# A graph layer's output product with the operands exchanged: rank sums stationary, W2 moving

## The chip, the cores and the metric

The kernel runs on one core of a Trainium2 chip. The metric is the device time of one execution in microseconds (us). A measurement of this kernel repeats within a fraction of a percent: the three runs of the kernel before lie between 972.28 and 972.99 us, with a median of 972.44 us.

Five engines work side by side, each on its own queue of instructions: TensorE (PE, with its weight loads listed apart as PEld), VectorE (DVE), ScalarE (ACT), GpSimd (POOL) and SyncE (SP, which here issues the DMAs). They wait for one another through semaphores.

## The reference

There are 128 graphs of 128 nodes with 64 features. The first layer is an edge network, the second a weighted sum over neighbours.

```python
# layer 0
h = relu(layernorm(x))                         # no scale, no shift
mask = (adj > 0)
t[b,j,k,:] = relu(h[b,j] @ W1a + (h[b,j] - h[b,k]) @ W1b + b1)   # 192 hidden channels
hm[b,j,:] = sum over k of t[b,j,k,:] * mask[b,j,k]
x1 = x + hm @ W2 + deg[b,j] * b2               # W2 is 192 x 64
# layer 1
h2 = relu(layernorm(x1))
out = x1 + (adj @ h2) @ W.T
```

The change touches `hm @ W2` and the addition that makes `x1` from it.

## The kernel before

**Groups and jobs.** The graphs are worked on in 32 groups of G = 4. In a group, each node's neighbours are ranked within each quarter of the 128 nodes, and the first D = 6 of a quarter get a slot. A *job* builds pre-activations for one half of the nodes (64) and two of the four quarters. `Job.fill` (L852) multiplies stacked projections `k3` by one-hot slots `S3` and adds the node's own part, into a PSUM tile `g`. `Job.drain` (L873) empties it. For the first 128 hidden channels (kind 0, one graph) DVE reduces the absolute values into `hm0` (L880). For the last 64 channels (kind 1, two graphs beside each other on the partitions) ACT writes the rectified values into `T` (L890), and POOL adds them up into `hm1`. A group has 24 jobs, numbered t = 0 to 23: 16 of kind 0 and 8 of kind 1; t = 4, 5, 10, 11, 16, 17, 22 and 23 are of kind 1. Edges that found no slot go another way (`pre_edge_*`, `edge_x`, `edge_sum`), through `et`, `R`, `RT` and `X`.

**What runs between the jobs.** While group g's jobs run, pieces for group g+1 (table `AHEAD`, L909) and for group g-1 (table `BEHIND`, L927) are put between them, at the job number that is their key. Those that matter here:

- `pre_proj(g+1, 0)` after t = 7 and `pre_proj(g+1, 1)` after t = 12 (L552): PE writes projections into a PSUM tile `pp`, which comes from the same three buffers as the jobs' `g`. ACT copies a first bfloat16 part (`ca<-pp`), makes `z` (four) and `e` (two); DVE forms `rest` from `pp` and that part; ACT makes the second part (`ca<-rest`); POOL the third (two `ca<-rest,ca`).
- `pre_edge_a` after t = 9: `pv` on PE, `ovf` and `mid` on DVE, four `et<-iov,mid` on ACT. `pre_edge_b` after t = 19: four `et<-et,half` and one `R<-et` on ACT.
- `edge_sum` after t = 1 and `edge_sum1` after t = 4: they end with `u0` (128 hidden channels x 4 graphs x 128 nodes) and `u1` (64 channels of two graphs on 128 partitions x 2 x 128 nodes), the sums over neighbours with hidden channels on the partitions.
- `post0` after t = 8 and `post1` after t = 10: described below. `post2` (L804, after t = 15): `sdb` on ACT, `rsb` and `mrb` on DVE, four `h<-x,mrb,rsb` on ACT. `post3` after t = 16: `pga` on PE and `agg` on ACT. `post4` after t = 19: `po` on PE, `ot` on DVE, the store.

**The product before.** `post0` (L769) holds `w2h` (half of W2's first 128 rows, 128 x 64) and `w2bd` (the last 64 rows twice on a block diagonal, 128 x 128) stationary and lets `u0` and `u1` move, 256 columns at a time. The product `py` then has output features on the partitions; ACT copies it to `ys` in SBUF. `post1` (L790) transposes `ys` twice on PE into `pty`, so that nodes are on the partitions, DVE adds `e` (which holds x and the parts that are linear in h) to give `x1`, and the sums of the layer norm follow (`stb`, `mvb`).

**Buffers.** `gtile` (L237) has 3 buffers of two PSUM banks each, shared by the jobs' `g` and by `pp`: a job can be filled only when a buffer has been drained. `mtile` (L240) has 2 buffers of one bank, for all the small products (`py`, `pty`, `pga`, `po`, `px` and others).

**What sets the order.** PE's instructions stand as they are written. After the first group's preparation `Engine.held` is set to False (L1016), and from there on a scheduler in the framework puts the instructions of DVE, ACT, POOL and SP in order when the program is built; each engine then works its list strictly from the front. The first group and the last have job orders of their own (L963 to L972); the 30 groups between them have the same one, and the built program has the same order of ACT's instructions in all 30.

The helpers `mm`, `tp` and `Engine.call` record every instruction, so that the profile gives nearly all of them the lines 181, 184 and 198; the tile names tell them apart.

Of the kernel before, what the change touches and what calls it, by code (L numbers as in the profile page):

```python
# [8 lines left out]
F32 = mybir.dt.float32  # L9
BF16 = mybir.dt.bfloat16  # L10
I32 = mybir.dt.int32
AF = mybir.ActivationFunctionType
ALU = mybir.AluOpType
# [137 lines left out]
def kernel(  # L151
# [28 lines left out]
    def mm(*args, **kw):  # L180
        return tc.keep_in_program_order(nc.tensor.matmul(*args, **kw))  # L181

    def tp(*args, **kw):
        return tc.keep_in_program_order(nc.tensor.transpose(*args, **kw))  # L184

    class Engine:
# [4 lines left out]
        def __init__(self, engine):  # L191
            self.engine = engine
# [10 lines left out]
    vec, act, pool, sp = (Engine(e) for e in (nc.vector, nc.scalar, nc.gpsimd, nc.sync))  # L203

    B, N, F = x.shape
    H = W1.shape[1]
    O = W2.shape[1]
    P = 128
    G = 4
# [18 lines left out]
    with ExitStack() as main:  # L228
# [4 lines left out]
        tmp = main.enter_context(tc.tile_pool(name="tmp", bufs=2))  # L233
# [3 lines left out]
        def gtile(name):  # L237
            return ps_g.tile([P, 2, 512], F32, tag="g", name=name)

        def mtile(name):  # L240
            return ps_m.tile([P, 512], F32, tag="m", name=name)
# [7 lines left out]
        w2bd = const.tile([P, 2, O], F32, tag="w2bd", name="w2bd")  # L249
        wl1 = const.tile([P, P], F32, tag="wl1", name="wl1")  # L250
        ident = const.tile([P, P], F32, tag="ident", name="ident")
# [20 lines left out]
        for q in range(Q):  # L272
            s = slice(q * QN, (q + 1) * QN)
# [35 lines left out]
        w2h = const.tile([C0, O], F32, tag="w2h", name="w2h")  # L309
# [69 lines left out]
        def bc(t, n, axis):  # L379
            shape = list(t.shape)  # L380
            shape.insert(axis, n)
            return t.unsqueeze(axis).to_broadcast(shape)


        def norm_a(src, u):
            st = tmp.tile([P, G, 6], F32, tag="st", name=f"st{u}")
            mv = tmp.tile([P, G, 2], F32, tag="mv", name=f"mv{u}")
            for b in range(G):
                vec.bn_stats(st[:, b, :], src[:, b, :])
            for b in range(G):  # L390
                vec.bn_aggr(mv[:, b, :], st[:, b, :])
            return mv
# [27 lines left out]
        def keep_busy(tile, n):  # L420
            for _ in range(n):
                mm(tile, oneb, bc(oneb, 4, 1), start=True, stop=True, skip_group_check=True)

        def pre_adj(g, busy=0):
            d = groups[g]
            pt = mtile(f"pt{g}")
            keep_busy(pt, busy)
            for b in range(G):
                tp(pt[:, b * N : (b + 1) * N], d["adj"][:, b, :], ident)
            d["adjT"] = grp.tile([P, G, N], F32, tag="adjT", name=f"adjT{g}", bufs=3)  # L430
            if g == 0:
                pre_norm(0)
            act.activation(
                d["adjT"].rearrange("k b j -> k (b j)"), pt, AF.Copy
            )
            if g < 2:
                return
            pre_mask(g)

        def pre_mask(g):  # L440
            d = groups[g]
            d["maskT"] = grp.tile([P, G, N], BF16, tag="maskT", name=f"maskT{g}", bufs=3)
            vec.tensor_scalar(d["maskT"], d["adjT"], 0.0, -1.0, ALU.is_gt, ALU.mult)
            if "mv" not in d:
                d["mv"] = norm_a(d["x"], f"a{g}")

        def pre_norm(g):
            d = groups[g]

            d["h"] = tmp.tile([P, 2, 2, F], F32, tag="h", name=f"h{g}", bufs=1)  # L450
            norm_b(d["x"], d["mv"], lambda b: d["h"][:, b % 2, b // 2, :], f"a{g}", d.get("scales"))

        def pre_rank(g, busy=0):
            d = groups[g]
            pq = mtile(f"pq{g}")
            keep_busy(pq, busy)
            mm(
                pq, triq, d["maskT"].rearrange("k b j -> k (b j)"), start=True, stop=True
            )
            d["qs"] = grp.tile([P, G, N], BF16, tag="qs", name=f"qs{g}")  # L460
            qf = d["qs"].rearrange("k b j -> k (b j)")
            act.activation(qf, pq, AF.Copy)

            d["ov"] = grp.tile([P, G, N], BF16, tag="ov", name=f"ov{g}")
            vec.tensor_scalar(d["ov"], d["qs"], float(D) + BIG, None, ALU.is_ge)
# [56 lines left out]
                d["hT"].rearrange("p r n -> p (r n)"), ph[:, 0 : 2 * N], AF.Copy  # L522
            )

        def pre_count(g, busy=0):
            d = groups[g]

            pd = mtile(f"pd{g}")
            keep_busy(pd, busy)
            for b in range(G):  # L530
                mm(
                    pd[:, b : b + 1], d["maskT"][:, b, :], negb, start=True, stop=True
                )
                mm(
                    pd[:, G + b : G + b + 1], d["ov"][:, b, :], oneb[:, 0:1], start=True, stop=True
                )
            d["dn"] = grp.tile([P, 2, G], F32, tag="dn", name=f"dn{g}")
            vec.tensor_copy(d["dn"].rearrange("j t b -> j (t b)"), pd[:, 0 : 2 * G])

            d["ns"] = grp.tile([P, G], F32, tag="ns", name=f"ns{g}")  # L540
            vec.scalar_tensor_tensor(
                d["ns"], pd[:, G : 2 * G], float(Q * D), d["dn"][:, 0], ALU.add, ALU.subtract
            )

            d["half"] = tmp.tile([P, G], F32, tag="half", name=f"half{g}")
            vec.tensor_scalar(
                d["half"], pd[:, G : 2 * G], -0.5, 0.5, ALU.mult, ALU.add
            )
            d["nb"] = tmp.tile([P, G], BF16, tag="nb", name=f"nb{g}")
            vec.tensor_copy(d["nb"], pd[:, G : 2 * G])  # L550
# [217 lines left out]

        def post0(g):  # L769
            d = groups[g]  # L770
            py = mtile(f"py{g}")
            d["py"] = py
            for p in range(2):
                s = slice(p * O, (p + 1) * O)
                mm(
                    py[s, 0 : 2 * N], w2h,
                    d["u0"][:, 2 * p : 2 * p + 2].rearrange("h r j -> h (r j)"),
                    start=True, stop=False, skip_group_check=True,
                )
            w = w2bd.rearrange("h p o -> h (p o)")  # L780
            mm(
                py[:, 0 : 2 * N], w, d["u1"].rearrange("h r j -> h (r j)"),
                start=False, stop=True, skip_group_check=True,
            )
            d["ys"] = tmp.tile([P, 2, N], F32, tag="ys", name=f"ys{g}", bufs=1)
            act.activation(
                d["ys"].rearrange("p r j -> p (r j)"), py[:, 0 : 2 * N], AF.Copy
            )

        def post1(g):  # L790
            d = groups[g]
            pt = mtile(f"pty{g}")
            for r in range(2):
                tp(pt[:, r * N : (r + 1) * N], d["ys"][:, r], ident)
            d["x1"] = grp.tile([P, G, F], F32, tag="x1", name=f"x1{g}")
            vec.tensor_tensor(
                d["x1"].rearrange("j (p r) o -> j r p o", p=2),
                pt[:, 0 : 2 * N].rearrange("j (r p o) -> j r p o", r=2, p=2),
                d["e"].rearrange("j (p r) o -> j r p o", p=2),
                ALU.add,  # L800
            )
            d["mv"] = norm_a(d["x1"], f"b{g}")

# [30 lines left out]


        class Job:
            def __init__(self, g, kind, b, jh, qp, busy):
                self.g, self.kind, self.b, self.jh, self.qp = g, kind, b, jh, qp
                self.gt = gtile(f"g{g}_{kind}_{b}_{jh}_{qp}")
                keep_busy(self.gt[:, 0], busy)  # L840

                if kind == 0:
                    self.parts = [(b, slice(0, C0), slice(0, P))]
                else:
                    self.parts = [
                        (2 * p + b, slice(C0, H), slice(p * C1, (p + 1) * C1)) for p in range(2)
                    ]
# [80 lines left out]
            0: (slot_sum,),  # L928
            1: (edge_sum,),
            4: (edge_sum1,),  # L930
            8: (post0,),
            10: (post1,),
            15: (post2,),
            16: (post3,),
            19: (post4,),
# [85 lines left out]
        for g in range(NG):  # L1021
            if 0 < g < NG - 1:
                load(g + 1)
            order = ORDER0 if g == 0 else ORDERL if g == NG - 1 else ORDER
            for t, args in enumerate(order):
                job = Job(g, *args, busy=0)
                job.fill()
                job.drain()
                if g == 0 and t in FIRST:
                    FIRST[t](0)  # L1030
                pieces(OWN, t, g)
                pieces(BEHIND, t, g - 1)
                pieces(AHEAD if g else AHEAD0, t, g + 1)
# [37 lines left out]
```

## Time and profile before

| | |
|---|---|
| median of three runs | 972.44 us |
| the profiled execution | 972.88 us |
| span of its instructions | 971.2 us, mean granted PE clock 0.994 |
| DVE busy | 796.4 us (82% of the span) |
| ACT busy | 698.9 us (72%) |
| POOL busy | 743.1 us (77%) |
| ACT `ys<-py` | 32 times, 0.427 us each at the median |
| one group, from one group's first `py` to the next one's | 474.88 to 504.01 us: 29.1 us |

How to read it. The span counts from the first instruction to the last; the time of the execution is a little longer. A row of the timeline has the start in us, the time from the first start to the last end of the merged instructions, the engine, the operation, the tiles written and read, the number merged, and in brackets the idle time before and what ended it. A matmul is listed with the time from its start until its result stands in PSUM; several overlap. So four `g<-id,k` matmuls are listed with 0.49 us together, while the next instruction begins 0.33 us after the first of them. A short wait of PE is covered by such an overlap and does not show as idle time; the starts have to be compared. For DVE and ACT, too, an instruction can begin about 0.1 us before the listed end of the one ahead of it.

### The profile page before, as it was taken

To read this page: it belongs to the slowest core of one execution; us is meant where nothing else is said; L and a number is where in the kernel's file an instruction comes from. 1 tells how busy PE (TensorE), PEld (TensorE's weight loads), DVE (VectorE), ACT (ScalarE), POOL (GpSimd) and SP (SyncE) were. 2 spreads that over 40 slices of the span, in tenths; PEclk is the share of its full clock that TensorE was granted. 3 is DMA by queue.
4 is the path that set the end of the run, shared out by engine and by line. 5 is a ranking of instruction groups with operands and counts; after the bars stand their busy time and mean duration, and the time that the engine had idled before them with its cause. 6 is when DMAs were issued, how large, how long until landed. Compare 5 with 4: busy or idle time off the path is not lost. (4 is left out here: it accounts for less than half of the span.)

```text
span 971.2 us, 26764 instructions
## 1 busy us (share of the span) xinstructions
PE 945.9 (97%) x10007; PEld 692.5 (71%) x10008; DVE 796.4 (82%) x1880; ACT 698.9 (72%) x1732; POOL 743.1 (77%) x1130
## 2 busy tenths in 40 slices
PE   6899999999999999999999999999999999999995
PEld 2667777777777767777777777777777777777774
DVE  6788888888888888888888888888888888888863
ACT  4867787767787767787767787767787767787752
POOL 1388787778787778787778787778787778787793
PEclk9999999999999999999999999999999999999998
DMA  3655676655676655676655676655676655666510
GB/s 99 132 128 126 150 166 137 148 128 124 145 165 144 138 127 128 147 163 144 138 128 128 146 163 137 145 129 127 146 164 144 140 126 126 147 154 138 123 46 14
DMA packets 88294, 129.91 MB, mean 134 GB/s; under 512 B 47200, under 2 KB 63968, under 8 KB 88160
## 3 DMA queue, kind: packets, MB, share of 16 engines
q1 hardware_dynamic: 87584, 127.98, 57.8%
q8 instruction: 81, 1.33, 0.6%
q14 instruction: 53, 0.43, 0.1%
q10 hardware_dynamic: 576, 0.16, 0.1%
HBM read 13.01 MB, written 4.19 MB: 18 GB/s over the span
## 5 line engine op out<-in xcount | busy, mean ns | idle before, releaser
L198 POOL TENSOR_TENSOR T<-T 128x192 f32<-128x192 f32 (+2 forms) x768 | 526.3, 692 | 97.2 <-ACT T L198 57.2
L198 DVE TENSOR_REDUCE hm<-g 128x64 f32<-128x768 f32 x512 | 476.8, 947 | 81.2 <-PE g L181 79.5
L181 PEld LDWEIGHTS <-k 96*128 96x128 bf16 (+1 forms) x6144 | 411.0, 103 | 177.1 <-issue 51.3
L181 PE MATMUL g<-S,k 96*128 96x384 bf16 (+1 forms) x2048 | 381.9, 330 | 4.7 <-DVE hm L198 3.5
L181 PE MATMUL g<-id,k 96*128 96x192 bf16 (+1 forms) x4096 | 379.8, 246 | 0.0
L198 ACT ACTIVATE T<-g 128x768 f32<-128x768 f32 x256 | 209.5, 820 | 74.5 <-PE g L181 70.2
L198 POOL TENSOR_TENSOR ca<-rest,ca 128x384 bf16<-128x384 f32 x126 | 112.5, 913 | 103.7 <-ACT ca L198 101.2
L198 ACT ACTIVATE ca<-pp 128x768 bf16<-128x768 f32 x64 | 51.4, 803 | 56.0 <-PE pp L181 56.0
L198 DVE TENSOR_TENSOR rest<-pp,ca 128x768 f32<-128x768 f32 x64 | 60.8, 949 | 14.6 <-ACT e L198 14.0
L198 ACT ACTIVATE ca<-rest 128x768 bf16<-128x768 f32 x64 | 55.2, 862 | 22.2 <-DVE rest L198 22.2
L198 DVE TENSOR_SCALAR S<-qs 128x512 bf16<-128x512 bf16 x186 | 71.0, 434 | 0.0
L181 PE MATMUL pe<-RT,X 128*64 128x128 f32 (+1 forms) x512 | 70.5, 280 | 0.0
L181 PE MATMUL pp<-wp,hT 64*128 64x448 f32 x256 | 67.0, 600 | 0.4 <-DVE bias L198 0.4
L198 ACT ACTIVATE z<-pp,ns 128x128 f32<-128x128 f32 (+1 forms) x256 | 65.9, 348 | 0.0
L198 ACT ACTIVATE et<-et,half 128x128 f32<-128x128 f32 x128 | 57.0, 449 | 0.0
L198 ACT ACTIVATE qs<-pq 128x512 bf16<-128x512 f32 x32 | 19.1, 597 | 52.2 <-PE pq L181 50.4
L181 PEld LDWEIGHTS pe<-RT,X 128*64 128x64 f32 (+1 forms) x512 | 52.7, 165 | 5.4 <-issue 5.4
L181 PE MATMUL px<-ca,S 128*128 128x192 bf16 x384 | 52.7, 246 | 0.0
L181 PE MATMUL px<-ca,R 128*128 128x192 bf16 x384 | 52.6, 246 | 0.0
L198 ACT ACTIVATE h<-x,mrb,rsb 128x64 f32<-128x64 f32 x128 | 51.6, 478 | 1.0 <-DVE mrb L198 1.0
L198 ACT ACTIVATE h<-x,mra,rsa 128x64 f32<-128x64 f32 x128 | 48.6, 432 | 1.8 <-issue 1.3
L181 PE MATMUL pe<-ident,z 128*128 128x128 f32 x192 | 49.6, 286 | 0.0
(128 smaller groups left out, 1208.3 us busy)
## 6 DMA issues: line engine op xcount, KB each, us to landing
S<-S SPq DMA_DIRECT2D x372, 192.0 KB, 4.1
k<-ca SPq DMA_DIRECT2D x384, 96.0 KB, 2.2
adj<-in_adj_dram SPq DMA_DIRECT2D x32, 256.0 KB, 3.0
x<-in_x_dram SPq DMA_DIRECT2D x32, 128.0 KB, 2.7
out_dram<-ot SPq DMA_DIRECT2D x32, 128.0 KB, 2.2
w<-in_L_gnn_W_dram SPq DMA_DIRECT2D x2, 96.0 KB, 4.5
bias<-in_L_gnn_b_dram ACTq DMA_DIRECT2D x1, 96.0 KB, 3.5
w2a<-in_L_gnn_W_dram ACTq DMA_DIRECT2D x1, 32.0 KB, 2.3
```

Source lines behind the costliest of these rows:

```text
L181: return tc.keep_in_program_order(nc.tensor.matmul(*args, **kw))
L198: ins = f(*args, **kw)
```

## The change

`post0` now makes the product with the operands exchanged. For each graph, `u0` (128 x 128) is stationary and `w2h` (64 columns) moves; for each pair of graphs, `u1` is stationary and `w2bd` (128 columns) moves. The result has nodes on the partitions at once. The copy `ys` and the two transposes into `pty` are gone, and `post1` adds `e` to `py` straight from PSUM. `post1` is called right after `post0`, at t = 8, and no longer at t = 10. The argument `busy`, which was 0 in every call of the kernel before, is taken out; it issued no instruction.

```diff
         def post0(g):
             d = groups[g]
-            py = mtile(f"py{g}")
-            d["py"] = py
-            for p in range(2):
-                s = slice(p * O, (p + 1) * O)
-                mm(
-                    py[s, 0 : 2 * N], w2h,
-                    d["u0"][:, 2 * p : 2 * p + 2].rearrange("h r j -> h (r j)"),
-                    start=True, stop=False, skip_group_check=True,
-                )
-            w = w2bd.rearrange("h p o -> h (p o)")
-            mm(
-                py[:, 0 : 2 * N], w, d["u1"].rearrange("h r j -> h (r j)"),
-                start=False, stop=True, skip_group_check=True,
-            )
-            d["ys"] = tmp.tile([P, 2, N], F32, tag="ys", name=f"ys{g}", bufs=1)
-            act.activation(
-                d["ys"].rearrange("p r j -> p (r j)"), py[:, 0 : 2 * N], AF.Copy
-            )
+            py = d["py"] = mtile(f"py{g}")
+            for b in range(G):
+                mm(
+                    py[:, b * O : (b + 1) * O], d["u0"][:, b], w2h,
+                    start=b == 0, stop=False, skip_group_check=True,
+                )
+            pyr = py[:, 0 : G * O].rearrange("j (p r o) -> j r p o", p=2, r=2)
+            for r in range(2):
+                mm(
+                    pyr[:, r], d["u1"][:, r], w2bd, start=False, stop=True, skip_group_check=True,
+                )
 
         def post1(g):
             d = groups[g]
-            pt = mtile(f"pty{g}")
-            for r in range(2):
-                tp(pt[:, r * N : (r + 1) * N], d["ys"][:, r], ident)
             d["x1"] = grp.tile([P, G, F], F32, tag="x1", name=f"x1{g}")
             vec.tensor_tensor(
-                d["x1"].rearrange("j (p r) o -> j r p o", p=2),
-                pt[:, 0 : 2 * N].rearrange("j (r p o) -> j r p o", r=2, p=2),
-                d["e"].rearrange("j (p r) o -> j r p o", p=2),
-                ALU.add,
+                d["x1"], d["py"][:, 0 : G * O].rearrange("j (b o) -> j b o", b=G), d["e"], ALU.add
             )
             d["mv"] = norm_a(d["x1"], f"b{g}")
...
-            8: (post0,),
-            10: (post1,),
+            8: (post0, post1),
```

More of the change, by code (lines that the diff above doesn't have):

```diff
@@ L422, in keep_busy, with pre_adj @@
                 mm(tile, oneb, bc(oneb, 4, 1), start=True, stop=True, skip_group_check=True)
-        def pre_adj(g, busy=0):
+        def pre_adj(g):
             d = groups[g]
             pt = mtile(f"pt{g}")
-            keep_busy(pt, busy)
             for b in range(G):
@@ L451, in pre_norm, with pre_rank @@
             norm_b(d["x"], d["mv"], lambda b: d["h"][:, b % 2, b // 2, :], f"a{g}", d.get("scales"))
-        def pre_rank(g, busy=0):
+        def pre_rank(g):
             d = groups[g]
             pq = mtile(f"pq{g}")
-            keep_busy(pq, busy)
             mm(
@@ L523, in pre_hT, with pre_count @@
             )
-        def pre_count(g, busy=0):
+        def pre_count(g):
             d = groups[g]
             pd = mtile(f"pd{g}")
-            keep_busy(pd, busy)
             for b in range(G):
@@ L836, with __init__ @@
         class Job:
-            def __init__(self, g, kind, b, jh, qp, busy):
+            def __init__(self, g, kind, b, jh, qp):
                 self.g, self.kind, self.b, self.jh, self.qp = g, kind, b, jh, qp
                 self.gt = gtile(f"g{g}_{kind}_{b}_{jh}_{qp}")
-                keep_busy(self.gt[:, 0], busy)
                 if kind == 0:
@@ L1025 @@
             for t, args in enumerate(order):
-                job = Job(g, *args, busy=0)
+                job = Job(g, *args)
                 job.fill()
```

## The prediction

> **What bounds the kernel now.** I read the page's busy shares first.
>
> ```profile
> PE 945.9 (97%) x10007; PEld 692.5 (71%) x10008; DVE 796.4 (82%) x1880; ACT 698.9 (72%) x1732; POOL 743.1 (77%) x1130
> ```
>
> PE looks like the bound. But its listed matmuls overlap, so this share hides waits below some 0.2 us. All steady groups look alike, so I took one, from 474.9 to 503.3 us, and asked for busy times in three stretches (columns: length; PE, PEld, DVE, ACT, POOL; clock; DMA).
>
> ```profile
> 474.90:477.40 2.50, 2.50 (x27) 1.72 (x26) 1.95 (x3) 1.75 (x8) 0.70 (x3) 1.00 1.00 202
> 477.40:488.50 11.10, 11.10 (x122) 8.24 (x119) 9.02 (x29) 11.10 (x31) 9.43 (x13) 1.00 0.82 187
> 488.50:503.30 14.80, 14.72 (x166) 11.02 (x165) 13.12 (x27) 8.17 (x16) 12.47 (x20) 1.00 0.38 92
> ```
>
> In the middle stretch ACT is busy for all of 11.10 us. Does that stretch hold PE up? The timeline of ACT there, then of PE:
>
> ```profile
> 477.40 0.84 ACT L198 ACTIVATE ca<-rest 128x768 bf16<-128x768 f32 x1 [0.75 <-DVE rest L198]
> ...
> 486.35 0.86 ACT L198 ACTIVATE T<-g 128x768 f32<-128x768 f32 x1
> 487.04 0.45 ACT L198 ACTIVATE agg<-pga 128x256 f32<-128x256 f32 x1
> 487.31 0.47 ACT L198 ACTIVATE et<-et,half 128x128 f32<-128x128 f32 x1
> 487.60 0.88 ACT L198 ACTIVATE T<-g 128x768 f32<-128x768 f32 x1
> 488.29 0.48 ACT L198 ACTIVATE et<-et,half 128x128 f32<-128x128 f32 x1
> 488.58 0.37 ACT L198 ACTIVATE sda<-mva,eps 128x4 f32<-128x4 f32 x1
> 488.80 0.76 ACT L198 ACTIVATE R<-et,ones 128x512 bf16<-128x512 f32 x1
> ```
>
> ```profile
> 487.27 0.49 PE L181 MATMUL g<-S,k 96*128 96x384 bf16 x2
> 487.59 0.49 PE L181 MATMUL g<-id,k 96*128 96x192 bf16 x4
> 487.92 0.64 PE L181 MATMUL po<-wl1t,agg 128*128 128x128 f32 x4
> 488.53 0.48 PE L181 MATMUL g<-S,k 96*128 96x384 bf16 x2
> ```
>
> It does. The `T` that starts at 486.35 (job 16) ends at 487.21, and job 19's fill begins at 487.27. The `T` at 487.60 (job 17) ends at 488.48, and job 20's fill begins at 488.53. Both times a fill begins 0.05 us after ACT has freed a buffer. After that ACT waits for PE again (8.17 busy of 14.80). So the period of 29.1 us is a loop: PE from job 20 to the next `pp`; ACT's `ca<-pp`, `z`, `e`; DVE's `rest`; 11.1 us of ACT in list order until job 17's `T`; job 20. `py`, `ys` and `pty` all lie beside the ACT part of this loop, not in it: `e` ends at 476.38 and `rest` starts at 476.41.
>
> ```profile
> 474.99 0.96 DVE L198 TENSOR_REDUCE hm<-g 128x64 f32<-128x768 f32 x1 [0.37 <-PE g L181]
> 476.41 0.96 DVE L198 TENSOR_TENSOR rest<-pp,ca 128x768 f32<-128x768 f32 x1 [0.46 <-ACT e L198]
> ```
>
> **PE's part of the change.** The old block runs from 474.88 (`py`) to 476.00 (next fill). The fill ahead of it ends at 474.79 (last `g<-id` at 474.70 plus its 0.08 step), so it takes 1.21. `pty` costs 0.36 (477.56 to 477.92) and about 0.1 ahead of it, 0.46. Together 1.67 us go. The new form is not in the trace, but `po` is its near twin: float32, 128 x 128 stationary, a new load for each pass, two passes for each matmul.
>
> ```profile
> 458.71 0.53 PEld L181 LDWEIGHTS po<-wl1t,agg 128*128 128x128 f32 x4
> L181 PEld LDWEIGHTS po<-wl1t,agg x128: 186/192/333, 79.9 to 965.6; 128*128 128x128 f32 x128
> ```
>
> Four loads span 0.53 and one is listed with 0.19, so a step is (0.53 - 0.19) / 3 = 0.112 us. The new block has 12 passes (4 x 2 with `u0`, 2 x 2 with `u1`): 1.34 us, and no gap ahead (`po` starts on the step). With 64 moving columns the stream alone would be half a step, so the lower bound is 8 x 0.056 + 4 x 0.112 = 0.90, if loads cost nothing. If a load could not run beside the matmul ahead of it, a pass would cost a load and a stream: 8 x 0.168 + 4 x 0.224 = 2.24, the upper bound. I take 1.34: two loads of `po` start within one listed load, and the shape of the load is the same. PE thus saves 1.67 - 1.34 = 0.33 us per group.
>
> The Trainium skill speaks against overlap here. Its page "TensorE: Matmul & The Clock Gate", Part 3, "What overlaps and what doesn't", says that weight loads run beside matmuls in flight only when their row groups differ, and all passes here use all rows. The `po` rows contradict it, since loads and matmuls of the same 128 rows step at 0.112; by the rule the sum would be the upper bound's.
>
> ACT loses `ys`, 0.43 us, which ended at 476.65 while ACT waited for `rest` until 477.40: worth nothing by itself. No DMA is added, dropped or moved past another.
>
> **The order of the other engines.** `post1` moves up, and the framework's scheduler makes new lists. From the built program's order, the same in all 30 middle groups:
>
> - DVE before: `hm` (job 8), `rest`, `hm` (9), `ovf`, `mid`, `x`, `stb`, `mvb`, `hm` (12). After: `hm` (8), **`x`**, `rest`, `stb`, `mvb`, `hm` (9), `ovf`, `mid`, `sta`, `hm` (12), `mva`, `rsb`, `mrb`.
> - ACT before, from `ca<-rest` to job 17's `T`: ca, T, et x4, T, sdb, et, ca, z x4, e x2, h x2, X x2, h x2, ca, X x2, et, T, agg, et, T. After: ca, T, T, et x4, sdb, **et x2, h**, ca, z x4, e x2, h, X x2, h x2, ca, X x2, **et x2**, T, agg, **R**, T. All that stood there still does, and one more `et` and `R`, which had come behind that `T`, now stand ahead of it.
>
> This is a new wait on DVE: `x` waits for the end of `py` and holds `rest`, `stb` and `hm` (9) behind it; ACT's `ca<-rest` waits for `rest`.
>
> **The walk through one group**, in the trace's own time, job 8's fill unchanged. `py` starts at 474.79, its last pass at 474.79 + 11 x 0.112 = 476.02; listed with 0.275 like `po`, plus 0.04 for DVE to see it: 476.33. `x` holds DVE for 0.33 (`ot`, same shape, 0.415, next one 0.33 after its start). `rest` starts at 476.66, not 476.41: **+0.25**. `ca<-rest` follows at 477.65. Then ACT's steps from start to start, from the rows: ca 0.75, T 0.69 twice, et x4 1.17, sdb 0.19, et x2 0.58. The next would be `h` at 481.72. But `h` needs `mrb`:
>
> ```profile
> L198 DVE SCALAR_TENSOR_TENSOR mrb<-mvb,rsb x32: 161/514/640, 73.1 to 962.0; 128x4 f32<-128x4 f32 x32
> L198 DVE SCALAR_TENSOR_TENSOR mra<-mva,rsa x32: 152/162/273, 4.9 to 899.4; 128x4 f32<-128x4 f32 x32
> 481.23 0.52 DVE L198 SCALAR_TENSOR_TENSOR mrb<-mvb,rsb 128x4 f32<-128x4 f32 x1
> 481.14 0.59 POOL L198 TENSOR_TENSOR T<-T 128x192 f32<-128x192 f32 x1
> ```
>
> The same tiny operation takes 0.16 as `mra` and 0.51 as `mrb`. In this group `mrb` ends at 481.75, just as the POOL add ends (481.73); I read it as held up by that add. Before, nothing waited for it. After: `sdb` starts at 480.95 and takes 0.29, `rsb` 0.18, so `mrb` starts at 481.48. POOL hangs on `ca<-rest` too and is 0.25 later; the add runs 481.39 to 481.98. So `h` starts at 482.03: **+0.31** (0 if the add misses it, the bound below). Then h 0.33, ca 0.69, z 0.89, e 0.40, h 0.33, X 0.42, h x2 0.66, ca 0.74, X 0.42, et x2 0.58, T 0.69, agg 0.27, R 0.65 (its 0.76 less the usual 0.1 overlap): 7.07. Job 17's `T` starts at 489.10 instead of 487.60: +1.50, which is 0.25 + 0.31 + **0.29** (et) + **0.65** (R). Job 20's fill slips from 488.53 to 490.03. PE cannot make it up, as its own work there ends earlier than before; what follows job 20 hangs on PE and shifts as a whole.
>
> 30 groups x 1.50 = 45.0 us. At the end, where no jobs cover it, the chain `py` (957.79) to `x` (960.08) took 2.29; now 11 x 0.112 + 0.275 + 0.04 = 1.55: -0.75. The last group's jobs with its own order have no `rest` or `et`; there 1.38 of PE go (`py` 938.49 to 939.65, `pty` 941.10 to 941.32) and 1.34 come: nothing. Sum +44.2. The span 971.2 becomes 1015.4, the profiled 972.88 becomes 1017, and against the median of 972.44 I forecast **1016.5 us**.
>
> **The rivals.**
> (a) *PE is the bound and the change saves its work.* One mechanism: ACT's list has slack, so job 20 follows PE alone. Then 32 x -0.33 - 0.75 = -11.3, 961. For it: 97% PE, and PE's own waits are small. Against it: ACT at 11.10 of 11.10, and the two fills 0.05 behind `T`. It decides once the two T ends come earlier than PE's arrival. Chance 0.06.
> (b) *Only the list order costs*: `py` at its lower bound is done before `rest` could start, and `mrb` misses the add. 30 x 0.94 - 0.75 = +27.5, 1000. With one of the two, 1007 to 1009. For it: 64 columns are a short stream. Against it: `po`'s load steps. Chance 0.20.
> (c) *Loads not hidden*: `py` 2.24, so `x` and `rest` come 0.90 later still than in my walk, 1.50 + 0.90 = 2.40 a group: 30 x 2.40 - 0.75 = +71, 1044. For it: no row has so short a stream behind such a load. Against it: `po`'s steps. Chance 0.05.
> (d) *It moves nothing*: the delay is absorbed in ACT's 6.6 us of waiting after job 20. But that waiting is for PE, which job 20 releases. Chance 0.03.
> The forecast and its near surroundings have 0.66.
>
> **How the numbers follow.** The forecast, 1009 to 1024, and (b) make up 0.86; the range is 1000 to 1030, the upper end for a group's delay near 1.9 us (between 1.50 and 2.40). A change of 0.2% (1.9 us) is about what can be told from none. Faster 0.06, same 0.03, slower 0.91 (0.66 + 0.20 + 0.05).
>
> **What would show it.** Right: a group period near 30.6 us; `rest` about 1.75 us after job 8's reduce starts; ACT idle little between `ca<-rest` and job 17's `T`, with `R` ahead of that `T`, and job 20's fill 0.05 behind its end; new `py` block 1.34; `h` behind an `mrb` of 0.5. Wrong: a period at or below 29.1, job 20's fill well behind the end of `T`, or loads of `py` stepping other than at 0.11.

## The result and the profile after

| | before | after |
|---|---|---|
| median, us | 972.72 (972.28 to 973.87, 4 runs) | 1025.74 (1024.74 to 1025.96, 4 runs) |
| span of the profiled execution, us | 971.2 | 1024.2 |
| one middle group, first `py` to next first `py`, us | 29.13 | 30.96 |

The changed kernel is slower: 1.0541 of the time before, 95% interval 1.0523 to 1.0559. The span grew by 53.0 us. From the first of the 32 `py` to the 30th there are 29 periods; they grew from 844.88 to 897.67 us, by 52.8. The rest is small: the 30th period is 1.68 longer and the last 0.03, the first `py` comes 0.70 earlier, and the stretch behind the last one is 0.73 shorter.

The page's busy shares of the changed kernel:

```profile
PE 942.2 (92%) x10135; PEld 718.5 (70%) x10136; DVE 790.4 (77%) x1880; ACT 692.5 (68%) x1700; POOL 737.3 (72%) x1130
```

PE, DVE, ACT and POOL each are busy for 3.7 to 6.4 us less than before, in a span 53 us longer. Only PE's weight loads, which overlap its matmuls, grew, by 26.0 us. So none of the four is busy for longer; their waits got longer. The stretches of one group that answer to those shown before (length; PE, PEld, DVE, ACT, POOL; clock; DMA):

```profile
499.65:502.50 2.85, 2.85 (x35) 2.58 (x33) 2.23 (x4) 1.60 (x7) 0.78 (x3) 1.00 1.02 205
502.50:514.85 12.35, 10.78 (x118) 8.13 (x115) 9.37 (x29) 12.09 (x33) 9.92 (x14) 1.00 0.72 165
514.85:530.60 15.75, 15.38 (x170) 11.48 (x170) 12.75 (x27) 7.83 (x15) 12.34 (x20) 1.00 0.38 88
```

All three are longer: 2.85 instead of 2.50, 12.35 instead of 11.10, 15.75 instead of 14.80. (The last stretch before ended at 503.30, 0.71 ahead of the next `py`; up to there it is 15.51.) In the middle one ACT is still nearly full (12.09 of 12.35), and now PE visibly isn't (10.78). The borders are set by eye, so the exact split comes from starts, below. ACT's timeline of the middle stretch, then PE's:

```profile
506.93 0.44 ACT L198 ACTIVATE h<-x,mrb,rsb 128x64 f32<-128x64 f32 x1 [0.21 <-DVE mrb L198]
...
511.81 0.74 ACT L198 ACTIVATE et<-et,half 128x128 f32<-128x128 f32 x2
512.40 0.86 ACT L198 ACTIVATE T<-g 128x768 f32<-128x768 f32 x1
...
513.35 0.79 ACT L198 ACTIVATE R<-et,ones 128x512 bf16<-128x512 f32 x1
513.96 0.88 ACT L198 ACTIVATE T<-g 128x768 f32<-128x768 f32 x1
```

```profile
513.31 0.48 PE L181 MATMUL g<-S,k 96*128 96x384 bf16 x2 [0.59 <-ACT T L198]
...
514.89 0.48 PE L181 MATMUL g<-S,k 96*128 96x384 bf16 x2 [0.29 <-ACT T L198]
```

Two `et` stand ahead of job 16's `T`, and `R` stands ahead of job 17's. That `T` ends at 514.84, and job 20's fill begins at 514.89. The waits of PE that were hidden in overlaps before now stand in brackets: 0.59 and 0.29 us, both for a `T`.

The start of the group: `py` on PE, then what DVE does with it.

```profile
499.66 1.03 PE L181 MATMUL py<-w2h,u 128*128 128x64 f32 x8
500.53 0.66 PE L181 MATMUL py<-w2bd,u 128*128 128x128 f32 x4
501.03 0.49 PE L181 MATMUL g<-S,k 96*128 96x384 bf16 x2
```

```profile
501.23 0.42 DVE L198 TENSOR_TENSOR x<-py,e 128x256 f32<-128x256 f32 x1 [0.41 <-PE py L181]
501.57 0.95 DVE L198 TENSOR_TENSOR rest<-pp,ca 128x768 f32<-128x768 f32 x1
```

`py` takes 501.03 - 499.66 = 1.37 us, and `rest` stands behind `x`, which waited 0.41 for `py`.

Medians over the middle groups, in us after a reference point: the end of job 8's fill, which is also the first pass of `py` after (before, `py` starts 0.09 behind it):

| | before | after | difference |
|---|---|---|---|
| `rest` starts | 1.62 | 1.91 | 0.29 |
| first `h<-x,mrb,rsb` starts | 8.37 | 7.27 | (moved in the list) |
| job 16's `T` starts | 11.56 | 12.74 | 1.18 |
| job 17's `T` starts | 12.81 | 14.30 | 1.49 |
| job 20's fill starts | 13.74 | 15.24 | 1.50 |
| from there to the next reference point | 15.39 | 15.72 | **0.33** |

The first part is what was forecast. The last row isn't: the stretch after job 20 did not merely shift, it became longer.

### The profile page after: what moved, and what is told of

Its sections match the earlier page's. It is cut to its first block, busy times and chain, and to the rows that moved or that the text cites. A ratio compares the mean times of both kernels' runs of the same rounds, so it can differ in the third digit from the quotient of the medians.

```text
span 1024.2 us, 26958 instructions
## 1 busy us (share of the span) xinstructions
PE 942.2 (92%) x10135; PEld 718.5 (70%) x10136; DVE 790.4 (77%) x1880; ACT 692.5 (68%) x1700; POOL 737.3 (72%) x1130
## 3 DMA queue, kind: packets, MB, share of 16 engines
q8 instruction: 82, 1.34, 0.6%
## 4 chain that ended last, share of the span: by engine, by line
PE 58%; ACT 22%; DVE 12%; issue 6%; DMA 1%; POOL 1%; SPq 0%; ACTq 0%; POOLq 0%; DVEq 0%
PE g L181 31%; ACT T L198 9%; PE pp L181 6%; PE px L181 6%; PE py L181 4%; ACT h L198 4%; DVE maskT L198 3%; PE pe L181 3%; DVE rest L198 3%; ACT et L198 2%; DVE u L198 2%; ACT R L198 2%; ACT X L198 2%; PE pga L181 2%; PE pj L181 1%
## 5 line engine op out<-in xcount | busy, mean ns | idle before, releaser
L198 POOL TENSOR_TENSOR T<-T 128x192 f32<-128x192 f32 (+2 forms) x768 | 521.0, 685 | 129.2 <-ACT T L198 89.3
L181 PEld LDWEIGHTS <-k 96*128 96x128 bf16 (+1 forms) x6144 | 417.0, 103 | 217.1 <-issue 103.1
L198 ACT ACTIVATE T<-g 128x768 f32<-128x768 f32 x256 | 206.4, 821 | 75.1 <-PE g L181 74.0
L198 ACT ACTIVATE h<-x,mrb,rsb 128x64 f32<-128x64 f32 x128 | 55.0, 471 | 6.8 <-DVE mrb L198 6.8
L198 DVE TENSOR_SCALAR maskT<-adjT 128x512 bf16<-128x512 f32 x32 | 33.3, 1041 | 23.2 <-ACT adjT L198 23.1
L198 POOL TENSOR_TENSOR hm<-T 128x64 f32<-128x64 f32 x128 | 40.7, 318 | 9.9
```

The costliest lines, as they stand in the source:

```text
L198: ins = f(*args, **kw)
```

## Experiments: one piece at a time

The kernel before ran beside each; ratios are to it. "Later than" and "earlier than" refer to the reference point above. An instruction of ACT or DVE can be held back in the built order with `tc.issue_after(...)`, which gives its list position a lower bound and adds no work.

**Put the lists back.** The last `et` and `R` of a group go behind job 17's `T`, as before the change. The layer norm's activations of the next group (`pre_norm`) are held behind `RT`, so that they don't fill the place.

```diff
+            if Engine.held or g < 2:
+                first, behind = G, ExitStack()
+            else:
+                first, behind = 3, tc.issue_after(groups[g - 1]["drain"].ins)
...
+            with behind:
...
+                d["R"] = grp.tile([P, G, E], BF16, tag="R", name=f"R{g}")
+                act.activation(d["R"], d["et"], AF.Relu, bias=ones[:, 0:1], scale=-1.0)
```

> The changed kernel with one thing put back: the last of the four et activations and R, which the scheduler had put ahead of job 17's T, are issued behind it (and the activations of the coming group's norm stay behind RT, so that nothing else slips forward). Product, x and all of DVE's list stay as changed. Theory (ACT's list between ca<-rest and job 17's T sets the period): T of job 16 comes 0.29 us earlier (one et less), T of job 17 0.94 earlier; PE then gets from job 19 through po to job 20 only 0.74 earlier than in the changed kernel, so 30 x -0.74 = -22, about 1003.5 us. Rival (the delay comes from DVE's x waiting for py, the list on ACT is only filler): no change, 1024 to 1027. Rival (PE's own new passes set the pace): no change either.

Measured: 992.46 us (991.29 to 993.93), ratio 1.0209 [1.0184, 1.0234]. Job 16's `T` comes 0.28 earlier than after the change, job 17's 0.89, job 20 0.74: these are the forecast places and sizes (0.29 for `et`; 0.89 - 0.28 = 0.61 for `R`, forecast 0.65). But the period fell by 1.16, to 29.79, and another 0.43 was gained behind job 20. One DVE instruction there had a new duration, `maskT`: 0.43 us here, 1.09 after the change and 0.76 before it. It was the suspect for the 0.33 in the table.

**Put `x` behind `rest`** on DVE, with the `pre_norm` hold of the run above.

```diff
+            ahead = groups.get(g + 2, {}).get("rest0")
+            with tc.issue_after(ahead.ins) if ahead else ExitStack():
+                vec.tensor_tensor(
+                    d["x1"], d["py"][:, 0 : G * O].rearrange("j (b o) -> j b o", b=G), d["e"],
+                    ALU.add,
+                )
```

> The changed kernel, but DVE issues rest ahead of x instead of behind it. With that the scheduler's ACT list has all four et but no R ahead of job 17's T. Theory (list): rest back by 0.25, R's 0.65 gone: T of job 17 0.90 earlier, T of job 16 0.25 earlier, PE reaches job 20 0.72 earlier than in the changed kernel: 30 x -0.72 = -22, about 1004 us; no gain from rest alone beyond that. Rival (x's wait for py is the whole cause): back to the kernel before, 970 to 975. Rival (PE's passes): 1024 to 1027.

Measured: 979.6 us (977.92 to 980.85), ratio 1.0085 [1.006, 1.011]: far below the expectation. ACT's timeline of this run at job 17's `T`, with the first `h` of the same group on top:

```profile
481.55 0.43 ACT L198 ACTIVATE h<-x,mrb,rsb 128x64 f32<-128x64 f32 x1
...
488.26 0.88 ACT L198 ACTIVATE T<-g 128x768 f32<-128x768 f32 x1
488.95 0.80 ACT L198 ACTIVATE R<-et,ones 128x512 bf16<-128x512 f32 x1
```

`h` has no wait in brackets any more, and `R` stands behind the `T` of job 17. So this edit took back three of the four terms, 0.29 of `x`, 0.30 of `mrb` and 0.61 of `R`: 1.20. Job 20 came at 14.03 in about half of the groups, 1.21 earlier, and at 13.81 in the others. In those others it is the reference point that had moved: the fill of job 8, whose end it is, had begun 0.36 later, behind a reduce on DVE. `maskT` took 0.47, and the period fell to 29.44. The expectation had counted `rest` and `R` (0.25 and 0.65), but not `mrb`, and it had job 16's `T` only 0.25 earlier, so that PE could bring job 20 no more than 0.72 forward. That `T` came 0.88 earlier, 0.29 by `rest`, 0.30 by `mrb` and 0.29 by one `et` that now stood behind it, and job 19's fill came 0.89 earlier. All four terms had been in the prediction; that the others depend on the first had not.

**Take `mrb` off the collision.** It becomes four operations with one input tensor in place of one with two.

```diff
-            vec.scalar_tensor_tensor(mr, mv[:, :, 0], -1.0, rs, ALU.mult, ALU.mult)
+            if u[0] == "b":
+                for b in range(G):
+                    vec.tensor_scalar(
+                        mr[:, b : b + 1], mv[:, b, 0:1], rs[:, b : b + 1], -1.0, ALU.mult, ALU.mult
+                    )
```

> The changed kernel with mrb made by four small DVE operations with one tensor operand each (the other factor is a per-partition scalar) instead of one with two tensors in SBUF; the lists of all engines are else the same. Theory (mrb of 0.51 us is held up by the POOL add that runs, and ACT's first h waits 0.21 to 0.31 us for it): each of the four takes under 0.2 us, h comes 0.1 to 0.3 earlier, 30 x -0.1 to -0.3: 1017 to 1023 us. Rival (mrb is slow for another reason, such as its own four-element read, or h's wait is not on the path): 1024 to 1028.

Measured: 1016.96 us (1013.68 to 1017.39), ratio 1.0467 [1.0441, 1.0492]. The first `h` starts 0.30 earlier and the period is 0.29 shorter, with `maskT` unchanged at 1.09. The term +0.31 is confirmed alone. For why the single operation is slow, compare in the changed kernel DVE's `mrb` and POOL's add beside it:

```profile
506.38 0.51 DVE L198 SCALAR_TENSOR_TENSOR mrb<-mvb,rsb 128x4 f32<-128x4 f32 x1
```

```profile
506.28 0.59 POOL L198 TENSOR_TENSOR T<-T 128x192 f32<-128x192 f32 x1
```

The add ends at 506.87, `mrb` at 506.89.

**Take `maskT` off the collision.** It reads the same numbers from PSUM (`pt`, which ACT copies to `adjT`) and no longer from SBUF.

```diff
-            vec.tensor_scalar(d["maskT"], d["adjT"], 0.0, -1.0, ALU.is_gt, ALU.mult)
+            src = d["adjT"] if pt is None else pt.rearrange("k (b j) -> k b j", b=G)
+            vec.tensor_scalar(d["maskT"], src, 0.0, -1.0, ALU.is_gt, ALU.mult)
```

> The changed kernel with maskT read from the transposed adjacency in PSUM instead of from its copy adjT in SBUF; the lists of all engines are the same. In the changed kernel maskT took 1.08 us where it took 0.76 before, and the next group's ph then stood 0.28 later behind it. Theory (a POOL add that now runs at that moment holds maskT up): read from PSUM it takes about 0.7 and needs not wait for adjT; ph comes 0.28 to 0.45 earlier: 30 x -0.28 to -0.45, 1012 to 1018 us. Rival (the extra 0.3 us per group comes from elsewhere): 1024 to 1028.

Measured: 1014.14 us (1011.17 to 1014.59), ratio 1.0438 [1.0413, 1.0463]. Job 20 stays at 15.25; the stretch behind it falls from 15.72 to 15.32, by 0.40, which is what `maskT` lost (1.09 to 0.69). So the part that the prediction had missed lies in this one instruction. DVE and POOL of the changed kernel, DVE and POOL of the run with the lists put back, and the group row of `maskT` in this run (duration min/median/max in ns, first and last start):

```profile
521.24 1.08 DVE L198 TENSOR_SCALAR maskT<-adjT 128x512 bf16<-128x512 f32 x1 [0.72 <-ACT adjT L198]
```

```profile
521.05 1.73 POOL L198 TENSOR_TENSOR T<-T 128x384 f32<-128x384 f32 x2
```

```profile
504.43 0.43 DVE L198 TENSOR_SCALAR maskT<-adjT 128x512 bf16<-128x512 f32 x1 [0.80 <-ACT adjT L198]
```

```profile
503.36 1.00 POOL L198 TENSOR_TENSOR T<-T 128x384 f32<-128x384 f32 x1
...
504.44 0.86 POOL L198 TENSOR_TENSOR T<-T 128x192 f32<-128x192 f32 x1
```

```profile
L198 DVE TENSOR_SCALAR maskT<-pt x30: 690/692/693, 52.6 to 940.1; 128x512 bf16<-128x512 f32 x30
```

In the changed kernel POOL's first add (the first of the two in the row, 1.00 us long) starts 0.2 ahead of `maskT`, and `maskT` ends 0.28 after that add. With the lists put back `maskT` starts in the gap between two adds, takes 0.43, and it is POOL's add that is long: 0.86, against 0.59 for the same form beside `mrb` above. Behind `maskT` on DVE stand a reduce and `u`, and PE's `ph` waits for `u`: that is the way into the period. The changed kernel's PE timeline has this wait, and the tables of waits have it for the weight load of `ph` (us in total, times, longest), first for the kernel before, then for the changed one:

```profile
523.84 0.44 PE L184 MATMUL ph<-ident,h 128*128 128x128 f32 x2 [0.33 <-DVE u L198]
```

```profile
PEld ph L184 <- DVE u L198: 8.7, 30, 0.3
```

```profile
PEld ph L184 <- DVE u L198: 18.5, 30, 0.6
```

The wait grew by 9.8 us in 30 groups, 0.33 a group, which is all of the missed part. In the other runs, too, the stretch behind job 20 follows `maskT` where that is long: 15.38 us with 0.76 (the kernel before), 15.37 with 0.74, 15.46 with 0.83 (these two from the position runs below), 15.71 with 1.09. At 0.66 and below it stays at 15.29, unless another wait adds to it.

**Product and lists separately.** The prediction's core claim is that the list order costs the time and the saved PE work is worth nothing. So one kernel has the new product with good lists (`post1` at job 10, `x` behind `rest`, all four `et` and `R` behind job 17's `T`, `pre_norm` behind `RT`) and one has the old product with the same lists.

```diff
+                first, behind = 0, tc.issue_after(groups[g - 1]["drain"].ins)
...
-            8: (post0, post1),
+            8: (post0,),
+            10: (post1,),
```

> The new product with x put back to job 10 and behind rest, and all four et and R issued behind job 17's T: the set ahead of that T is then three et smaller than in the kernel before. ACT's and DVE's lists are those of its twin with the old product, but for ys. Theory (list): T of job 17 0.88 us earlier than in the kernel before; PE then sets the pace, 0.33 us per group of it saved by the product and 0.24 between job 17 and job 20: 30 x -0.57 = -17, about 955 us. Rival (the new product itself is slow): above 972.

> The old product, with all four et and R issued behind job 17's T; lists else as in its twin with the new product. Theory (list): the kernel before was held by ACT's list; with 0.88 us less ahead of job 17's T, PE reaches job 20 0.24 earlier and then is the bound: 30 x -0.24 = -7, about 965 us. The difference to the twin is the product alone: 0.33 us a group, 10 us. Rival (the kernel before was bound by PE): no change, 971 to 974.

Measured: 965.69 us (963.76 to 966.13), ratio 0.9931 [0.9919, 0.9943], with the new product, 966.3 (966.03 to 967.79), ratio 0.9939 [0.9926, 0.9951], with the old one. Both beat the kernel before. The intervals overlap: with equal lists the product itself is worth nothing that can be measured, where 10 us had been expected of it. The run with the old product came out near its forecast of 965; the one with the new product missed its 955. Both periods are 28.84. DVE of the run with the new product shows where PE's saved time goes, then PE:

```profile
472.02 0.41 DVE L198 TENSOR_TENSOR x<-py,e 128x256 f32<-128x256 f32 x1
...
473.00 0.36 DVE L198 BATCH_NORM_AGGREGATE mvb<-stb 128x2 f32<-128x6 f32 x4
473.28 0.92 DVE L198 TENSOR_REDUCE hm<-g 128x64 f32<-128x768 f32 x1
```

```profile
474.25 0.48 PE L181 MATMUL g<-S,k 96*128 96x384 bf16 x2 [0.25 <-DVE hm L198]
```

Job 13's fill waits for job 12's reduce, which ends at 474.20. DVE has no idle time ahead of that reduce, so PE, though earlier, waits there: from the first `pp` to the next fill 1.38, with the old product 1.12.

**Position and product separately, without touching the lists.** The old product with `post1` at job 8, and the new product with `post1` at job 10; each moves one line.

```diff
-            8: (post0,),
-            10: (post1,),
+            8: (post0, post1),
```

> The kernel before with its old product, copy and transposes, but post1 called right after post0 at job 8: the position alone. The scheduler's list then has one more et ahead of job 17's T (not R), and pty waits for ys on PE. Theory (list): 0.29 for the et, and job 10's T about 0.65 later since PE stands until ys: up to 30 x 0.94 = 28, 981 to 1001 us. Rival (the new operands are the cause, not the position): 970 to 975.

> The changed kernel with post1 back at job 10: the new product alone, the old position. The list has neither a further et nor R ahead of job 17's T, but x still stands before rest, and the last h comes after the second pair of X. Theory (list): rest 0.25 late; pga has to wait for the last h, which holds PE about 1.0 us a group: up to 30 x 1.0 = 31, 980 to 1003 us. Rival (the product alone, without list effects, saves PE's 0.33 a group): about 961.

Measured: 1000.47 (1000.15 to 1000.56), ratio 1.0287 [1.0272, 1.0303], and 997.74 us (996.14 to 998.34), ratio 1.0257 [1.024, 1.0274]. Either half alone costs 25 to 28 us, for the most part by a wait of PE that the changed kernel doesn't have. In the first, PE's written order has `pty` right behind `py`, and PE waits there for `ys`. This and one more `et` (0.29) make job 17's `T` 0.89 later, with a period of 30.00. In the second, `rest` starts at 1.91, as after the change: `post1` is written later, and yet `x` still stands ahead of `rest` and waits for `py`. But job 17's `T` is only 0.27 later by that, while job 20 is 0.84 later and the period 0.91 longer. Most of the rest is a wait of PE for the last `h`, which ACT's list has behind the second pair of `X`, as the expectation had it. PE's rows of the first run and of the second:

```profile
518.78 0.44 PE L184 MATMUL pty<-ident,ys 128*128 128x128 f32 x2 [0.54 <-ACT ys L198]
```

```profile
527.52 0.32 PE L181 MATMUL pga<-adjT,h 128*64 128x128 f32 x1 [0.60 <-ACT h L198]
```

The 961 us of the rival in which PE is the bound are not reached by any of these versions.

**Is DVE at job 13 the whole floor?** The good lists, with `post1` at job 12, so that job 12's reduce stands behind `x` and two `stb` only, and no longer behind four `stb` and four `mvb`; and the same with `maskT` from PSUM.

```diff
-            10: (post1,),
+            12: (post1,),
```

> As the run with the new product and all et and R behind job 17's T, but post1 at job 12, so that the reduce of job 12 stands on DVE behind x and two stb only, no longer behind x, four stb and four mvb. ACT's list is the same. In that run job 13's fill began 0.05 us after the reduce of job 12 ended, 0.32 us after PE was ready. Theory (PE's saved 0.33 a group was lost in that wait): job 13 begins 0.3 earlier, period about 28.5 us, 28.84 - 0.3, in all 953 to 959 us. Rival (another wait behind it, on DMA or ACT, takes its place): 963 to 967.

> The same, with maskT read from PSUM as well. Theory (maskT of 0.66 us behind adjT holds ph): it still takes 0.69 but starts earlier; ph comes 0.1 to 0.2 earlier, 3 to 6 us less than its twin. Rival (ph then waits for u behind the edge sum, which ends no earlier): the same as its twin.

Measured: 965.36 us (960.45 to 966.55), ratio 0.9923 [0.9901, 0.9946], and 965.81 (962.64 to 968.51), ratio 0.9933 [0.9912, 0.9954]. Job 13's fill did come 0.26 earlier (5.46 against 5.72), but of this only 0.13 was left at job 15 and at job 20, and behind job 20 it was lost (15.46 against 15.29 at the median). Another wait takes the place of the one removed, as the rival had it. The tables of waits name it, first with `post1` at job 10, then at job 12 (us in total, times, longest):

```profile
PEld L181 <- DMA k<-ca: 1.4, 5, 0.3
```

```profile
PEld L181 <- DMA k<-ca: 5.6, 18, 0.6
```

So with `post1` at job 12 PE's weight loads of `k`, for the first jobs of the next group, wait 18 times instead of 5 for the DMAs that fill `k`. The second edit had nothing to take away: in the first run `maskT` met no add and took 0.43 already (17 of 18 groups), and from PSUM it took 0.69. What the whole floor near 28.8 us consists of stays open: no single wait accounts for it in these runs.

**Add work to PE.** Job 18 multiplies its first products three times, the last result standing: 4 more matmuls, some 0.65 us a group, on the changed kernel and on the one before.

```diff
-                job.fill()
+                job.fill(3 if t == 18 and 0 < g < NG - 1 else 1)
...
-                    for b, us, rows in self.parts:
+                    for b, us, rows in self.parts * times:
```

> The changed kernel with more work on PE: in job 18 of each middle group the four slot matmuls... two of them, 384 columns each, are issued three times instead of once (each restarts the sum, so the result is the same): four more matmuls of 0.163 us, 0.65 us a group. All engines' lists are the same. Theory (PE waits 0.77 us between the fills of jobs 18 and 19 for job 16's T on ACT): the added work fits into the wait, no change, 1023 to 1028 us. Rival (PE's own work is the bound of the changed kernel): 30 x 0.65 = +20, about 1045 us.

> The same four added matmuls in the kernel before. There PE waits only 0.07 us ahead of job 19 and 0.16 ahead of job 20. Theory: 0.65 - 0.07 - 0.16 = 0.42 us a group appear, 30 x 0.42 = 12.6, about 985 us. Rival (PE alone is the bound of the kernel before): 30 x 0.65 = 19.6, 992 us. Rival (ACT has much slack to give): no change.

On the changed kernel: 1026.43 us (1025.14 to 1027.02), ratio 1.0556 [1.0537, 1.0575], against 1.0541 without the extra work. It fits into PE's wait ahead of job 19, as its PE timeline shows:

```profile
512.55 1.15 PE L181 MATMUL g<-S,k 96*128 96x384 bf16 x6
...
513.98 0.48 PE L181 MATMUL g<-S,k 96*128 96x384 bf16 x2
...
515.56 0.49 PE L181 MATMUL g<-S,k 96*128 96x384 bf16 x2 [0.30 <-ACT T L198]
```

Six matmuls stand where there were two; the wait of 0.59 ahead of job 19 is gone, and job 20's fill still waits for `T`, at the same 15.25. PE is not what sets job 20 in the changed kernel.

On the kernel before: 998.69 us (996.76 to 1000.72), ratio 1.0276 [1.0251, 1.0301], more than expected. Job 20 came 0.45 later, near the 0.42 forecast. The other 0.50 a group lies behind job 20 and not where the work was added. There the scheduler had put `rsa` ahead of job 18's reduce; it waits for `sda` on ACT, and DVE stood still:

```profile
500.16 0.18 DVE L198 RECIPROCAL rsa<-sda 128x4 f32<-128x4 f32 x1 [3.51 <-ACT sda L198]
```

So this run had another list, and says of PE's slack before only the 0.45. That the 0.50 comes from `rsa` is argued, since no run took it away alone.

## Why the prediction was right, and where it was off

1. *What bounds the kernel.* Right. Job 20's fill still begins 0.05 us behind job 17's `T`; 0.65 us more of PE work changed nothing; every gain in the experiments came from the order on ACT and DVE or from a held DVE operation; the losses of the two position runs came in part from waits of PE for ACT (`ys`, `h`). Rival (a), PE as the bound, falls, and with it (d): ACT's waiting after job 20 absorbed none of the delay.

2. *The new product.* 1.34 forecast, 1.37 measured. Rival (c), loads not hidden at 2.24, falls. The weight loads step as read from `po`: eight loads of `py` span 0.97 us and one is listed with 0.19, (0.97 - 0.19) / 7 = 0.111. The four loads for 128 moving columns span 0.53, a step of 0.113: the shorter stream of 64 columns bought nothing here. The lower bound of 0.90 falls too, and with it half of rival (b).

3. *`rest` behind `x`.* +0.25 forecast, +0.29 measured. The block was 0.03 longer than forecast.

4. *`h` behind a held `mrb`.* +0.31 forecast, 0.30 by the experiment that split it. Rival (b)'s other half, that `mrb` misses the add, falls.

5. *One more `et`, and `R`, ahead of job 17's `T`.* +0.29 and +0.65 forecast, 0.28 and 0.61 measured by putting them back. The sum at job 20, +1.50 forecast, is +1.50 measured. That it is so exact is in part luck: `rest` cost 0.04 more than forecast and `R` 0.04 less.

6. *"What follows job 20 hangs on PE and shifts as a whole."* This is the step that failed. It shifted, and became 0.33 us a group longer. The walk took every duration behind job 20 from the rows of before; `maskT` was one of them, at 0.76, and came out at 1.09 = 0.76 + 0.33. The same collision that the prediction had read from `mrb` and priced there hit a second DVE operation, whose neighbour on POOL the walk never looked up. In numbers: the mis-sized term is the stretch behind job 20, taken as 0 per group and measured as 0.33, and 30 x 0.33 = 9.9 of the 53.0 us. Without it the measured growth is 43.1, beside a forecast of 44.2. The range held because its upper end left room for a delay near 1.9 a group; the delay was 1.83, but no reason given there was this one.

7. *The ends.* From the last `py` to the last `x`: 1011.58 to 1013.22, 1.64 us, against 2.29 before: -0.65, forecast -0.75. The period of the last group was forecast unchanged and changed by 0.03. The first `py` came 0.70 earlier, which was not forecast and whose cause was not tried.

In these runs the four terms were not independent. Moving `x` alone took three of them back, since `mrb` and `R` had come where they were through the same new order.

## What to carry to other kernels

An edit that removes work from a full engine is worth nothing while a list on another engine releases it; compare the lists before and after, and walk one group instruction by instruction through the loop that sets the period. When one operation in the trace is found to be held by a neighbour on another engine, go through all other operations of that kind in the period and ask where each will stand against its neighbour once things shift. To judge a new formulation, give the old one the same order: here both reached 966 us, and the order was the whole of the gain.

## What the runs showed of the hardware

DVE's `maskT` (float32 from SBUF, bfloat16 to SBUF) took from 0.43 to 1.11 us with the same shape. In the 18 steady groups compared of each run, it ended 0.28 us after the end of the POOL add that was running at its start (0.29 in a few groups), whether it had started 0.12, 0.19, 0.40 or 0.53 us into that add. Where no add had started ahead of it, it took 0.43, and an add that started with it was the longer one: 0.86 in place of 0.59. Read from PSUM it took 0.69, and the add beside it kept its 1.00.

The Trainium skill's page "SBUF — State Buffer", section "SBUF: two separate sides", describes this: VectorE and GpSimd share a pair of SBUF ports as an exclusive lock, which whichever comes first keeps for its whole instruction, VectorE's side being an operation in a two-port mode or one with two SBUF inputs. The rows agree in three ways: both directions were seen, the hold lasts to the end of the add, and the PSUM source escapes it; `mrb`, with its two SBUF inputs, shows it too (0.51 beside an add, ending 0.02 us after it, and 0.16 in the last group without one). That `maskT` from SBUF runs in such a mode is argued from 0.43 against 0.69, not shown in a record.

So the choice between the two sources depends on the neighbour: 0.69 from PSUM beat 0.76 and 1.09 from SBUF, and loses to 0.43 and 0.66.
